# Seven block products for the output product of the 64-wide heads, and normed rows kept in DRAM

## The chip, the core and the metric

The kernel runs on one core of one Trainium2 chip. The metric is the device time of one execution in microseconds (us); the time of a kernel is the median of its runs.

## What is computed

The reference is a decoder of two layers on `x` of 8 entries x 256 rows x 256 columns, all in 32-bit floats. Each of six stages adds its result to `x`, and each works on the row-normed `x`. The change touches the last two stages:

```python
# fifth stage: cross attention, 16 heads of 64, 256 keys of a context plus one null key
q = _split_heads(x_normed @ Wq); k, v = split(context @ Wkv)      # plus the null key and value in front
attn = softmax(q * scale @ k.T)
out = (attn @ v) merged to 1024 columns
out = out @ Wout                                                   # 256 x 1024 times 1024 x 256, per entry
x = x + layernorm(out, 1e-6) * ln_scale + ln_bias
# sixth stage: one of 8 experts per row, and a shared expert for all rows, on the normed x
x = x + silu(x_n @ ws1) * (x_n @ ws3) @ ws2 + routed(x_n)
```

## The kernel before

Tensors are kept with 128 partitions. `x` stays in SBUF as 16 tiles of 128 rows. An entry is two such tiles.

The fifth stage (`null_cross_attention`) is a loop over the 8 entries. For entry b, TensorE forms the scores (`stx`), ScalarE their exponentials (`pTx`), TensorE the value products (`ox`) and the sums (`den`), and the result stands transposed in `oT`, 1024 columns of the heads as 8 chunks of 128 partitions by 256 tokens. Beside it, keys, values and queries for entry b + 1 are made by `seven`, which forms a 2 x 2 block product as seven block products with Strassen-like sums. Its two PSUM banks, `xb` and `yb`, are summed into and read several times on the way; a third, `zb`, is used once. The sums of the weights (`tw`, `twq`) are made once at the start of the stage by `sums_of_weights`; the sums of the rows (`sw`, `swq`) once per entry by `sums_of_rows`. The generators `k7`, `v7` and `q7` yield after each block product, so that they can be interleaved by hand.

The division of `oT` by the sums goes through DRAM: VectorE makes the reciprocals, four small DMAs on SP write them (`rd`), two DMAs of 512 KB read them back repeated over partitions (`rs`), and `divide` multiplies on GpSimd (in the last entry on GpSimd and VectorE). Then `outward` forms the output product as a plain product: per token tile, one null-value product and eight chunk products into one `mm` buffer, read by one copy:

```python
for t in range(2):
    product(ps[:, t, :], en[:, cols], nvw, True, False)
    for c in range(nc8):
        product(ps[:, t, :], oT[:, c, cols], wout_x[:, c, :], False, c == nc8 - 1)
nc.scalar.copy(y, ps)
```

`product` issues one matmul for each half of 64 output partitions; the profile records two passes for each. After `outward` come the norm statistics of `y`, the affine part, and the sum into `x`.

For the sixth stage each entry's finished `x` is normed (`routed_norm`), turned (`routed_rows`) into its slice of one tile `xnTe` (16 KB on each partition, in the pool `ws` opened before the stage) and multiplied by the router (`routed_scores`). In the last entry there are no keys to make, so the pools of the projection (`wproj`: the context tile, `wkv_x` and `wq_x`, the keys `kT` and values `vx`, the weight sums) are closed. `load_shared` then opens the pool `mids` in their place and loads the shared expert's weights `ws13`; `w_out` loads `ws2`. TensorE fills the place of the seven products with the first hidden products of the shared expert, `hx` (`hidden_shared(0)`, six steps, on rows 0 and 1 of `xnTe`), four of them ahead of the last `outward` and two behind it. `hidden_seven` follows for rows 2 and 3.

The order on TensorE is written out by hand within `manual_schedule`; on VectorE, ScalarE, GpSimd and SP a scheduler chooses it in this stage, and every engine and DMA queue works in order. PSUM here has three buffers `mm` of one bank, two buffers `sc` of two banks (`stx`, the bank pairs of `seven`, `hx`) and one for `den`. A tile reuses memory only once all users of what stood there have ended.

Of the kernel before, what the change touches and what calls it, by code (L numbers as in the profile page):

```python
# [29 lines left out]
F32 = mybir.dt.float32  # L30
# [4 lines left out]
ALU = mybir.AluOpType  # L35
# [122 lines left out]
def plain(  # L158
# [123 lines left out]
    def transposed(rows, work, mm, tag, dst=None, bufs=2):  # L282

        ps = mm.tile([P, 2, 2 * P], F32, tag="mm", name="tr")
        for t in range(2):
            for c in range(2):
                nc.tensor.transpose(ps[:, c, t * P : (t + 1) * P], rows[:, t, c * P : (c + 1) * P], ident)
        if dst is None:
            dst = work.tile([P, 2, 2 * P], F32, tag=tag, name=tag, bufs=bufs)
        nc.scalar.copy(dst, ps)  # L290
        return dst
# [815 lines left out]
    def w_in(pool, src1, src3, name):  # L1107

        t = pool.tile([P, 2, 2 * FF + tail], F32, name=name, tag=name)
        nc.sync.dma_start(t[:, :, :FF], src1.rearrange("(c p) f -> p c f", p=P))  # L1110
        nc.sync.dma_start(t[:, :, FF + tail :], src3.rearrange("(c p) f -> p c f", p=P))
        nc.gpsimd.tensor_copy(t[:, :, FF : FF + tail], t[:, :, 2 * FF :])
        return t

    def ended(t):

        nc.gpsimd.memset(t[tail:, full, :], 0.0)
        return t
# [12 lines left out]
    def load_router():  # L1131
        router = pool_s.tile([P, 2, E], F32, name="router")
        nc.gpsimd.dma_start(router, a["L1_ffn_router_DE"].rearrange("(c p) e -> p c e", p=P))
        shared.update(router=router, xnT=pool_s.tile([P, 2, B * S], F32, name="xnTe"))

    def load_shared(pool):

        shared["ws13"] = w_in(pool, a["L1_ffn_ws1_DF"], a["L1_ffn_ws3_DF"], "ws13")

        shared["mid_s"] = [ended(pool.tile([P, NFC, 2 * S], F32, name=f"mid{i}")) for i in range(2)]  # L1140
        shared["ws2"] = ended(pool.tile([P, NFC, D], F32, name="ws2"))

    def hidden(mid, first, n, pair, silu):

# [134 lines left out]
        return xn  # L1279

    def routed_rows(b, xn, work):
        transposed(xn, work, mm, "", shared["xnT"][:, :, bass.ts(b, S)])

    def routed_scores(b):

        ps = mm.tile([P, 2, D], F32, tag="mm", name="sc")
        for t in range(2):
            for c in range(2):
                product(
                    ps[:, t, :E], shared["xnT"][:, c, bass.ts(2 * b + t, P)], shared["router"][:, c, :], c == 0, c == 1  # L1290
                )
        nc.vector.tensor_copy(sc[:, 2 * b : 2 * b + 2, :], ps[:, :, :E])  # L1292

# [76 lines left out]
    def null_cross_attention(phase):  # L1370
# [18 lines left out]
        def w_blocks(w, m, extra):  # L1389

            v = w.rearrange("p (j c) (m k f) -> p j c m k f", j=2, m=m, k=2)
            blocks = [[v[:, j, :, :, k, :] for k in range(2)] for j in range(2)]
            t1, t2, t4 = (extra[:, i] for i in range(3))
            return blocks, (t1, t2, blocks[0][1], t4)
# [2 lines left out]
        kv_blocks = w_blocks(wkv_x, 2, wsum.tile([P, 3, *shape], F32, name="tw"))  # L1397
        shape = D // P // 2, 1, XH * XD // 2
        q_blocks = w_blocks(wq_x, 1, wsum.tile([P, 3, *shape], F32, name="twq"))

        def sums_of_weights(blocks, which):
            ((b11, b12), (b21, b22)), (t1, t2, t3, t4) = blocks
# [5 lines left out]
        def w_terms(blocks, m):  # L1408

            ((b11, b12), (b21, b22)), (t1, t2, t3, t4) = blocks  # L1410
            return [t[:, :, m, :] for t in (b11, b21, b22, t4, t1, t2, t3)]

        def sums_of_rows(rows, n, name, apart):


            def block(i, j):
                return rows[:, n * j : n * (j + 1), bass.ts(i, P)]

            sw = wsum.tile([P, 4 if apart else 3, n, P], F32, tag=name, name=name)
            s1, s2, s4 = (sw[:, i] for i in range(3))  # L1420
            s3 = sw[:, 3] if apart else block(1, 0)
            nc.vector.tensor_tensor(s1, block(1, 0), block(1, 1), ALU.add)
            nc.vector.tensor_tensor(s2, s1, block(0, 0), ALU.subtract)
            nc.vector.tensor_tensor(s4, block(0, 1), s2, ALU.subtract)
            nc.vector.tensor_tensor(s3, block(0, 0), block(1, 0), ALU.subtract)
            return block(0, 0), block(0, 1), s4, block(1, 1), s1, s2, s3
# [182 lines left out]
                    oT[:, c2 : c2 + 2, :], oT[:, c2 : c2 + 2, :], rs[:, c2 : c2 + 2, :], ALU.mult  # L1609
                )  # L1610

        def outward(b, oT, en):
            y = work.tile([P, 2, D], F32, tag="y", name="yx", bufs=1)
            ps = mm.tile([P, 2, D], F32, tag="mm", name="wo")
            for t in range(2):
                cols = bass.ts(t, P)
                product(ps[:, t, :], en[:, cols], nvw, True, False)
                for c in range(nc8):
                    product(ps[:, t, :], oT[:, c, cols], wout_x[:, c, :], False, c == nc8 - 1)
            nc.scalar.copy(y, ps)  # L1620
            mv, rs = norm_stats([y[:, t, :] for t in range(2)], 1e-6, small, "lx")
            for t in range(2):
                xt = x[:, 2 * b + t, :]
                normed(y[:, t, :], y[:, t, :], mv, rs, t)
                nc.vector.tensor_tensor(y[:, t, :], y[:, t, :], lns, ALU.mult)
                nc.vector.tensor_tensor(y[:, t, :], y[:, t, :], lnb, ALU.add)
                nc.gpsimd.tensor_tensor(xt, xt, y[:, t, :], ALU.add)
# [14 lines left out]
        (kT, v), qT = kv0, query_room()  # L1642
        sums_of_weights(kv_blocks, slice(0, 3))
        sums_of_weights(q_blocks, slice(0, 3))
        en = null_key(xnT)
        features(qT, wq_x, xnT, nc.vector.tensor_copy)
        for blocks in (kv_blocks, q_blocks):
# [3 lines left out]
        for b in range(B):  # L1651
            more = b + 1 < B
            if more:
                ctxT = context(b + 1)
            oT, den, rest = weighted(kT, v, qT)
            if more:
                _, xnT = layernorm_T(b + 1, work, mm, 1)
                if b:
                    xe = routed_norm(b - 1, work)
                of_ctx = sums_of_rows(ctxT, CTX // P // 2, "sw", False)  # L1660
            else:
                xe = routed_norm(b - 1, work)
                rest()

                wproj.close()
                late = ctx.enter_context(tc.tile_pool(name="mids", bufs=1, side="right"))
                tables = ctx.enter_context(tc.tile_pool(name="route", bufs=1, side="right"))
                load_shared(late)
                sums = phase.enter_context(tc.tile_pool(name="sums", bufs=1, side="right"))
                order.enter_context(tc.manual_schedule(engines={mybir.EngineType.PE}))  # L1670
            if more:
                order.enter_context(tc.manual_schedule(engines={mybir.EngineType.PE}))
            if b:
                routed_rows(b - 1, xe, work)
            if more:
                of_x = sums_of_rows(xnT, 1, "swq", True)
                kT, v, qT = key_room(), value_room(), query_room()
                k7 = seven("k7", of_ctx, w_terms(kv_blocks, 0), kT, False)
                v7 = seven("v7", of_ctx, w_terms(kv_blocks, 1), v, True)
                q7 = seven("q7", of_x, w_terms(q_blocks, 0), qT, False)  # L1680
                next(k7)
                rest()
            rs, old = reciprocals(b, den, en), en
            if b == 1:
                in_range()
            if not more:
                w_out(shared["ws2"], a["L1_ffn_ws2_FD"])
                routing_tables(tables)
            if more:

                for made in (k7, k7, v7, k7, k7, k7, v7, v7, q7, v7, q7, v7, v7, q7):
                    next(made)
            else:
                first = hidden_shared(0, pair, lambda n: spare()[:, 0, :n])
                for i in range(4):
                    next(first)
                    if i == 0:
                        routed_scores(b - 1)
                shared["of_w"] = sums_of_shared(*(sums.tile([P, full * P], F32, name=f"tws{i}") for i in range(4)))
            divide(oT, rs, (nc.gpsimd, nc.gpsimd if more else nc.vector))  # L1700
            outward(b, oT, old)
            if more:
                next(q7), next(q7)
                if b:
                    routed_scores(b - 1)
                next(q7)
                en = null_key(xnT)
            else:
                for _ in first:
                    pass  # L1710
            order.close()
# [1230 lines left out]
```

## Time and profile before

| | us |
|---|---|
| Median of 3 runs | 1150.59 (1148.03 to 1150.82) |
| The profiled execution's own time | 1146.4 |
| Its span | 1144.7 |
| Its mean granted TensorE clock | 0.993 of full |
| TensorE matmul busy | 1106.4 (97%) |
| VectorE, ScalarE, GpSimd busy | 581.4, 444.9, 418.8 |
| First matmul of the fifth stage to the first of the expert stage | 439.1 to 923.0 |

The span runs from the first to the last recorded work of the execution; 1.7 us lie around it. A timeline line gives the start and the duration in us, the engine, the source line, the operation, output<-input by the program's names, and the number of instructions merged into it. Matmuls are pipelined, so a line's duration runs a little beyond the start of the next. `SPq` is the queue that SP issues DMAs from. A window line gives its bounds and length, busy time and count for each engine, the granted clock, the DMA engines' share and GB/s.

### The profile page before, as it was taken

To read this page: it belongs to the slowest core of one execution; us is meant where nothing else is said; L and a number is where in the kernel's file an instruction comes from. 1 tells how busy PE (TensorE), PEld (TensorE's weight loads), DVE (VectorE), ACT (ScalarE), POOL (GpSimd) and SP (SyncE) were. 2 spreads that over 40 slices of the span, in tenths; PEclk is the share of its full clock that TensorE was granted. 3 is DMA by queue.
4 is the path that set the end of the run, shared out by engine and by line. 5 is a ranking of instruction groups with operands and counts; after the bars stand their busy time and mean duration, and the time that the engine had idled before them with its cause. 6 is when DMAs were issued, how large, how long until landed. Compare 5 with 4: busy or idle time off the path is not lost.

```text
span 1144.7 us, 33720 instructions
## 1 busy us (share of the span) xinstructions
PE 1106.4 (97%) x14690; PEld 704.9 (62%) x14690; DVE 581.4 (51%) x1577; ACT 444.9 (39%) x699; POOL 418.8 (37%) x480
## 2 busy tenths in 40 slices
PE   6979999999999999999999999999999999999997
PEld 3434455555555445767676767676765667888874
DVE  5557889899878447343433333332324573222213
ACT  4757776656444432232323323232414220222320
POOL 2427366446677422324141414142425223000014
PEclk9989999999999999999999999999999999999999
DMA  8073333231103200101010101010103026799934
GB/s 246 2 240 121 105 107 96 71 112 54 37 11 143 109 3 19 40 19 39 20 40 19 39 20 40 19 39 19 40 20 95 1 94 262 312 415 386 390 107 141
DMA packets 52253, 117.15 MB, mean 102 GB/s; under 512 B 8816, under 2 KB 37216, under 8 KB 47744
## 3 DMA queue, kind: packets, MB, share of 16 engines
q1 hardware_dynamic: 45920, 99.17, 25.4%
q0 software_dynamic: 3456, 12.73, 3.1%
q10 hardware_dynamic: 2720, 3.02, 0.7%
q8 instruction: 117, 1.92, 0.7%
q14 instruction: 40, 0.33, 0.1%
HBM read 104.26 MB, written 27.93 MB: 115 GB/s over the span
## 4 chain that ended last, share of the span: by engine, by line
PE 86%; DVE 6%; ACT 3%; issue 1%; SPq 1%; DMA 1%; POOL 1%; ACTq 0%; DVEq 0%; POOLq 0%
PE h L272 7%; PE st L330 7%; PE k L272 7%; PE v L272 6%; PE wo L272 5%; PE o L367 5%; PE ox L1553 5%; PE stx L1513 5%; PE out L1930 4%; PE out L1747 4%; PE qk L278 3%; PE h L1161 3%; PE q L272 3%; ACT pT L341 2%; PE ao L278 2%; PE v L278 2%
## 5 line engine op out<-in xcount | busy, mean ns | idle before, releaser
L341 ACT ACTIVATE pT<-st 128x1024 f32<-128x1024 f32 (+1 forms) x128 | 110.5, 915 | 74.2 <-PE st L330 70.3
L367 PE MATMUL o<-pT,padv 128*32 128x256 f32 (+1 forms) x1536 | 96.4, 367 | 7.0 <-DVE by_q L383 5.5
L1519 POOL TENSOR_TENSOR both<-pTx 128x512 f32<-128x512 f32 x64 | 81.5, 1298 | 27.1 <-issue 23.8
L272 PE MATMUL h<-xrT,w 128*64 128x128 f32 (+1 forms) x1936 | 87.1, 250 | 0.5 <-issue 0.5
L272 PEld LDWEIGHTS h<-xrT,w 128*64 128x64 f32 x1936 | 84.6, 137 | 3.4 <-issue 1.1
L341 ACT ACTIVATE pT<-st,kbias 128x1024 f32<-128x1024 f32 x64 | 67.9, 1112 | 36.0 <-PE st L330 36.0
L1154 DVE TENSOR_TENSOR midr<-sl,h 128x128 f32<-128x128 f32 x102 | 29.4, 288 | 100.7 <-PE h L272 67.5
L367 PEld LDWEIGHTS o<-pT,padv 128*32 128x32 f32 x1536 | 44.6, 110 | 54.4 <-issue 18.9
L1517 ACT ACTIVATE pTx<-stx 128x1024 f32<-128x1024 f32 x64 | 62.1, 1022 | 40.7 <-PE stx L1513 35.7
L1153 ACT ACTIVATE sl<-h 128x128 f32<-128x128 f32 (+1 forms) x114 | 35.4, 311 | 94.8 <-PE h L272 55.8
L330 PE MATMUL st<-qm,kT 32*128 32x512 f32 (+1 forms) x512 | 67.3, 594 | 3.7 <-DVE seq L513 2.2
L254 POOL TENSOR_TENSOR lnrs<-lnve,mhalf 128x2 f32<-128x2 f32 x48 | 35.8, 749 | 91.8 <-DVE lnve L252 84.9
L278 PE MATMUL qk<-xnT,l_wqkv 128*32 128x256 f32 x1024 | 68.5, 391 | 0.0
L1513 PE MATMUL stx<-qTx,kTx 64*128 64x256 f32 x512 | 64.3, 391 | 2.5 <-ACT pTx L1517 2.5
L1553 PE MATMUL ox<-pTx,vx 128*32 128x256 f32 x1024 | 62.3, 380 | 0.0
L1608 POOL TENSOR_TENSOR oT<-oT,rs 128x512 f32<-128x512 f32 x30 | 37.7, 1287 | 65.7 <-DMA rs<-rd 65.7
L1513 PEld LDWEIGHTS stx<-qTx,kTx 64*128 64x128 f32 x512 | 46.1, 186 | 20.7 <-ACT pTx L1517 7.2
L272 PE MATMUL wo<-wout_x,oT 128*64 128x256 f32 x512 | 58.0, 379 | 0.0
L346 POOL TENSOR_SCALAR_AFFINE_SELECT pT<-pT 128x512 f32<-128x512 f32 x64 | 42.1, 672 | 41.4 <-ACT pT L341 41.1
L254 POOL TENSOR_TENSOR lxrs<-lxve,mhalf 128x2 f32<-128x2 f32 x8 | 5.6, 704 | 133.5 <-DVE sc L1292 103.3
L278 PEld LDWEIGHTS qk<-xnT,l_wqkv 128*32 128x32 f32 x1024 | 32.9, 113 | 26.9 <-issue 8.7
L1930 PE MATMUL out<-w,midr 128*64 128x256 f32 x408 | 47.5, 379 | 0.7 <-issue 0.7
(365 smaller groups left out, 2154.8 us busy)
## 6 DMA issues: line engine op xcount, KB each, us to landing
w<-packs SPq DMA_DIRECT2D x22, 1408.0 KB
w<-packs SPq DMA_DIRECT2D x22, 768.0 KB
rs<-rd SPq DMA_DIRECT2D x16, 512.0 KB
packs<-L_ffn_w_eDF SPq DMA_DIRECT2D x8, 704.0 KB
packs<-L_ffn_w_eDF SPq DMA_DIRECT2D x8, 640.0 KB
packs<-L_ffn_w_eFD SPq DMA_DIRECT2D x8, 640.0 KB
wkv_x<-L_xattn_Wkv POOLq DMA_DIRECT2D x1, 4096.0 KB, 16.9
ctxT<-ctx_T SPq DMA_DIRECT2D x8, 512.0 KB
```

Of the source, the lines that this page charges most:

```text
L272: nc.tensor.matmul(out[h], lhsT[:, h], rhs, start=start, stop=stop, skip_group_check=True)
L278: nc.tensor.matmul(out[h : h + HP], lhsT[:, h : h + HP], rhs, start=start, stop=stop, skip_group_check=True)
L330: nc.tensor.matmul(st[:, r, :, :n], self.kT[rows, c, bass.ts(kt, P)], self.qm[rows, :, c, q0:], start=True, stop=True,)
L341: nc.scalar.activation(pT[:, :, :, :n], st[:, 2 * k : 2 * k + 2, :, :n], AF.Exp, scale=self.scale, **kb)
L346: nc.gpsimd.affine_select(out=pT[:, :, :, :P], in_=pT[:, :, :, :P], compare_op=ALU.is_ge, fill=0.0, base=0, pattern=[[0, 2], [0, 2], [1, P ...
L367: nc.tensor.matmul(o[HP * j : HP * j + HP, m, q0:], self.v_pad[:, kt, 8 * c + 2 * j + m, :], pTs[j // 2][:, j % 2, m, : S - q0], start=kt ...
L1513: nc.tensor.matmul(st[:, g, kt, :], kT[rows, c, bass.ts(kt, P)], qT[rows, c, :], start=True, stop=True)
L1517: nc.scalar.activation(pT, st, AF.Exp, scale=scale)
L1519: nc.gpsimd.tensor_tensor(both, pT[:, :, 0, :], pT[:, :, 1, :], ALU.add)
L1553: nc.tensor.matmul(o[at : at + HP, i, :], v[:, kt, 2 * (c2 + i) + g, lo : lo + HP], pT[:, g, kt, :], start=kt == 0, stop=kt == 1, skip_gro ...
L1747: nc.tensor.matmul(ps, mid[:, i, lo : lo + P], w2[:, i, :], start=i == 0, stop=i == NFC - 1)
L1930: nc.tensor.matmul(ps[h], mid[:, i, h], sets[k % len(sets)][1][:, i, :], start=i == 0, stop=i == NFC - 1, skip_group_check=True,)
```

## The change

The output product of each entry is made as seven products of blocks of 128 tokens x 512 inner columns x 128 output columns, in place of the eight that a plain product takes. The sums of the weight blocks (`two`, 16 VectorE sums of 128x128, with four of them written in place into `wout_x`) are made once at the start of the stage; the sums of the row blocks (`swo`, one of them in place in `oT`) once per entry on VectorE. The null-value products go into blocks 2, 5, 3 and 4, with the difference `ed` of two halves of `en` for block 3. The blocks use one `sc` buffer (`xb`, `yb`) and one `mm` buffer (`zb`), with three small copies on ScalarE, three sums on VectorE, and a last copy. Between blocks 7 and 4 stands one product of other work, `between()`: a step of `q7`, or in the last entry the fifth hidden step.

The turned normed rows of entries 0 to 5 go into a small tile `xnk` and from it to a DRAM tile `xt`, 256 KB each, on SP's queue. The tile `xnTe` is opened in the pool `mids` in the last entry, and six DMAs on SP bring the rows back, after the two of `ws13`. Entries 6 and 7 are copied straight into it. In that pool the two `mid` tiles are now opened first.

```diff
 def load_router():
-    shared.update(router=router, xnT=pool_s.tile([P, 2, B * S], F32, name="xnTe"))
+    shared["router"] = router
+xt = dram.tile([B - 2, P, 2, S], F32, name="xt")
+rows_of = {}
 def load_shared(pool):
+    mids = [pool.tile([P, NFC, 2 * S], F32, name=f"mid{i}") for i in range(2)]
     shared["ws13"] = w_in(pool, a["L1_ffn_ws1_DF"], a["L1_ffn_ws3_DF"], "ws13")
-    shared["mid_s"] = [ended(pool.tile([P, NFC, 2 * S], F32, name=f"mid{i}")) for i in range(2)]
-    shared["ws2"] = ended(pool.tile([P, NFC, D], F32, name="ws2"))
+    ws2 = pool.tile([P, NFC, D], F32, name="ws2")
+    xnT = pool.tile([P, 2, B * S], F32, name="xnTe")
+    for b in range(B - 2):
+        nc.sync.dma_start(xnT[:, :, bass.ts(b, S)], xt[b])
+    shared["mid_s"] = [ended(t) for t in mids]
+    shared["ws2"], shared["xnT"] = ended(ws2), xnT
 def routed_rows(b, xn, work):
-    transposed(xn, work, mm, "", shared["xnT"][:, :, bass.ts(b, S)])
+    if b < B - 2:
+        rows_of[b] = transposed(xn, work, mm, "xnk", bufs=1)
+        nc.sync.dma_start(xt[b], rows_of[b])
+    else:
+        rows_of[b] = transposed(xn, work, mm, "", shared["xnT"][:, :, bass.ts(b, S)])
...
+shape = nc8 // 2, 1, D // 2
+o_blocks = w_blocks(wout_x, 1, work.tile([P, 3, *shape], F32, name="two", bufs=1))
...
-def outward(b, oT, en):
+def outward(b, oT, en, between):
+    s_terms = sums_of_rows(oT, nc8 // 2, "swo", False, work)
+    t_terms = w_terms(o_blocks, 0)
...
+    nc.gpsimd.tensor_tensor(ed, en[:, :P], en[:, P:], ALU.subtract)
+    xy = scp.tile([P, 2, 2 * S], F32, tag="sc", name="wo")
+    xb, yb = xy[:, 0, :P], xy[:, 1, :P]
+    zb = mm.tile([P, 2 * S], F32, tag="mm", name="woz")[:, :P]
...
+    kept = work.tile([P, 3, P], F32, tag="pT", name="wok", bufs=4)
+    p1, p5, u = (kept[:, i] for i in range(3))
+    product_of(1, xb, True)
+    reads(xb, nc.scalar.copy(p1, xb))
+    product_of(2, zb, True, (e1, n1))
+    nc.vector.tensor_tensor(y[:, 0, :P], p1, zb, ALU.add)
+    product_of(5, yb, True, (e2, n2))
+    reads(yb, nc.scalar.copy(p5, yb))
+    product_of(6, xb, False)
+    reads(xb, nc.scalar.copy(u, xb))
+    product_of(3, yb, False, (ed, n2))
+    nc.vector.tensor_tensor(y[:, 0, P:], u, yb, ALU.add)
+    product_of(7, xb, False)
+    reads(xb, nc.vector.tensor_tensor(y[:, 1, P:], p5, xb, ALU.add))
+    between()
+    product_of(4, xb, False, (e2, n1))
+    nc.scalar.copy(y[:, 1, :P], xb)
...
 sums_of_weights(q_blocks, slice(0, 3))
+sums_of_weights(o_blocks, slice(0, 4))
 en = null_key(xnT)
 features(qT, wq_x, xnT, nc.vector.tensor_copy)
...
-outward(b, oT, old)
+outward(b, oT, old, lambda: next(q7 if more else first))
 if more:
-    next(q7), next(q7)
+    next(q7)
```

## The prediction

> **What bounds it.** I read the page's busy shares and chain first, then the timeline of each engine around the edited stage, then the order and waits of the changed program as built.
>
> ```profile
> PE 1106.4 (97%) x14690; PEld 704.9 (62%) x14690; DVE 581.4 (51%) x1577; ACT 444.9 (39%) x699; POOL 418.8 (37%) x480
> PE 86%; DVE 6%; ACT 3%; issue 1%; SPq 1%; DMA 1%; POOL 1%; ACTq 0%; DVEq 0%; POOLq 0%
> ```
>
> TensorE is busy 97% of the span and is 86% of the chain. In the stage of the heads of 64 (439 to 922 us) it hardly idles, so one us of TensorE removed there is worth one us, and one us of TensorE idleness added costs one. The timeline of TensorE, first in entry 0, then at the output product of entry 1:
>
> ```profile
> 470.23 3.66 PE L272 MATMUL k<-sw,tw 128*64 128x128 f32 x64
> 473.73 1.89 PE L272 MATMUL v<-wkv_x,ctxT 128*64 128x512 f32 x8
> ```
> ```profile
> 553.12 0.60 PE L272 MATMUL wo<-nvw,en 128*64 128x256 f32 x4
> 553.55 3.62 PE L272 MATMUL wo<-wout_x,oT 128*64 128x256 f32 x32
> 557.00 0.60 PE L272 MATMUL wo<-nvw,en 128*64 128x256 f32 x4
> 557.43 3.62 PE L272 MATMUL wo<-wout_x,oT 128*64 128x256 f32 x32
> 560.89 1.92 PE L272 MATMUL q<-swq,wq_x 128*64 128x128 f32 x32
> ```
>
> Columns: start, duration, engine, line, operation, count. Starts give the pitch: 64 matmuls of 128 columns take 473.73 - 470.23 = 3.50 us, 54.7 ns each; the 72 of the output product, 256 columns wide, take 560.89 - 553.12 = 7.77 us, 107.9 ns each.
>
> **Part 1, the product itself.** 7 block products x 4 chunks x 2 column halves x 2 recorded passes are 112 matmuls, the four null-value blocks 16 more: 128 x 54.7 ns = 7.00 us. That is 0.77 us less in each of 8 entries: **-6.2 us**. Against this the Trainium skill, page "TensorE: Matmul & The Clock Gate", section "Back-to-back issue gap", gives about 81 ns for a sustained 128-column matmul with its weight load; by it 128 would take 10.4 us and each entry would lose 2.6 us. The row above is for the same shape in the same loop, and decides.
>
> What the blocks need lies beside other work. In entry 1 the division by the sums ends on GpSimd at 543.06; the built order puts the first of the four row sums on VectorE (128x512, 0.60 to 0.69 us like the other 512-wide sums) just behind it, ahead of `vx<-v7p,v7z`, which slips from 541.24 to about 543.8. Behind it on VectorE the next copy was due at 547.35, and nobody on TensorE waits for the slipped one (three buffers in `mm`). The other sums end near 546.2, while the first block starts at 553.12: cost nothing; without the gap of 547.35 it would be 2.5 us an entry. The first block reuses the bank pair of `v7`, whose last copy ends at 553.05: 0 to 0.1 us an entry, I take 0. Each later bank read has a whole block product (0.87 us) between it and the next write of that bank; small copies take 0.3 us. `between()` puts one `q` product ahead of block 4, and the last `q` product no longer waits 0.38 us for `qTx` in entry 0: **-0.4 us** with entry 0 alone. The store of normed rows stands on SP between `ctxT` and `rd`; the rows are copied by 525.26, a sibling 256-wide issue takes about 0.5 us, `rd` is issued at 529.37: nothing.
>
> **Part 2, the sums of `wout_x` at the start of the stage.** Sixteen VectorE sums of 128x128 now stand ahead of the first `qTx` copy:
>
> ```profile
> 439.98 8.76 PE L272 MATMUL fm<-xnT,wq_x 128*64 128x256 f32 x64
> 448.68 2.00 PE L1513 MATMUL stx<-qTx,kTx 64*128 64x256 f32 x16
> ```
> ```profile
> 444.85 0.69 DVE L1406 TENSOR_TENSOR twq<-wq_x 128x512 f32<-128x512 f32 x1
> 445.45 0.69 DVE L1384 COPY qTx<-fm 128x512 f32<-128x512 f32 x1
> ```
>
> The fourth `fm` tile needs the first's buffer. Before, that copy came at 445.45 to 446.14, and the fourth tile began near 448.75 - 1.73 = 447.0 with no idleness. After: 444.85, three `twq` sums at 0.60 us, sixteen small ones at 0.20 to 0.31 us (starts of the `swq` rows at 466.77 to 467.49; I take 0.23, most do not depend on their neighbour), then the copy of 0.69: 444.85 + 1.8 + 3.7 + 0.7 = 451.05. TensorE idles **4.05 us** (3.5 to 5.3).
>
> An idle TensorE costs more than the gap. The windows of the first us, with the granted clock third from last:
>
> ```profile
> 18.00:20.00 2.00, 0.04 (x4) 0.04 (x4) 1.90 (x6) 1.43 (x3) 0.62 (x2) 1.00 1.09 367
> 20.00:22.00 2.00, 2.00 (x12) 0.50 (x16) 1.86 (x10) 0.98 (x4) 0.00 (x0) 0.54 1.09 351
> 22.00:24.00 2.00, 2.00 (x25) 0.89 (x24) 0.31 (x2) 1.88 (x2) 0.70 (x1) 0.60 1.10 358
> 24.00:26.00 2.00, 2.00 (x28) 0.72 (x24) 0.40 (x1) 1.10 (x3) 0.00 (x0) 1.00 1.02 376
> ```
>
> After 2.15 us of idleness the clock is about a half for some 3.8 us of work; the same shows after the 5.50 us wait that ends at 81.12 (half until 85.0) and after the short stalls at 436.6 to 439.1 (half from 440.0 to about 443.8). So each new gap of this size costs about 3.8 x 0.5 = **1.9 us** more, and nothing where the gap misses. The skill's page, section "Part 1: The HAM clock gate", has a window of about 3.4 us to fall and to recover, which would make this 1.7 us; the trace fell after a shorter gap. Part 2: 4.05 + 1.9 = **+6.0 us**.
>
> **Part 3, the shared rows in entry 7.** `xnTe` moves into the pool of the shared expert, beside `ws13` and ahead of it the two `mid` tiles. The pool grows past the region of `wkv_x` into that of `kT` and `vx`. In the program as built, the load of `ws13` waits for the last value product (`ox`) of entry 7; before, it waited for a `q` product of entry 6 and was issued here:
>
> ```profile
> 855.33 0.40 SPq L1110 DMA_DIRECT2D ws<-L_ffn_ws_DF  x1
> ```
> ```profile
> 872.50 1.91 PE L1553 MATMUL ox<-pTx,vx 128*32 128x256 f32 x32
> 874.22 0.61 PE L1528 MATMUL den<-both,hot 128*32 128x256 f32 x8
> 874.77 0.66 PE L287 MATMUL tr<-ident,xne 128*128 128x128 f32 x4
> 875.26 3.60 PE L1161 MATMUL hx<-xnTe,ws 128*128 128x512 f32 x8
> ```
>
> `ox` ends near 874.4; the hidden product `hx`, which needs `ws13` and rows 0 and 1 of `xnTe`, stands at 875.26. So 20 us of cover are gone. The price, from the load of before, by windows (last column GB/s):
>
> ```profile
> 855.00:857.00 2.00, 2.00 (x42) 1.83 (x40) 1.43 (x6) 0.19 (x1) 1.50 (x4) 1.00 0.20 41
> 857.00:859.00 2.00, 2.00 (x20) 1.45 (x18) 1.51 (x5) 0.98 (x3) 0.45 (x1) 1.00 0.92 329
> 859.00:861.00 2.00, 1.68 (x16) 1.05 (x14) 1.12 (x4) 1.74 (x2) 1.47 (x2) 1.00 1.03 405
> ```
>
> By 861 they sum to 2 x (41 + 329 + 405) = 1550 KB; `ws13` is 1442 KB, there 5.4 us after issue. Rows 0 and 1 are 524 KB in 1 KB pieces, like `ctxT` (325 GB/s in its best us): 1.6 us. Landing to use is 0.7 us (`ctxT` ends near 555.35 and is used at 556.07). Ready at 874.45 + 5.4 + 1.6 + 0.7 = 882.15: **6.9 us** idle (5 to 8.5), then the half clock, **1.9 us**.
>
> `rd` and `rs` stand on SP behind these loads and wait for their semaphores: `rd` complete near 885.5, `rs` behind rows 2 to 5 and `ws2` starts near 887, and moves 5 us as before, landing near 893; the division lets block 1 start at 894.5 and block 2 at 896. TensorE, with 4 hidden steps (14.5 us) and the slow clock, arrives at 898.6: nothing, but 0 to 4 us if that queue is slower. In the tail the sixth hidden step waits for `mid` of the fifth, one block of 1.09 us ahead instead of 7.8 us of product: 0.2 + 0.6 + 0.65 - 1.09, about **0.5 us**. The last rows' norm has 9.6 us for a chain of about 8.5: nothing.
>
> **Sum.** -6.2 - 0.4 + 6.0 + 6.9 + 1.9 + 0.5 = **+8.7 us**: on the profiled execution's span of 1144.7, 1153.4; its own time of 1146.4 becomes 1155.1. The three timed runs have their median 4.2 us above that execution; I add the change to the median: 1150.6 + 8.7 = **1159.3 us**. What a measurement can tell from no change is 0.3%, 3.5 us.
>
> **Rivals.** A (not slower): the last stage's loads cost little. If they land within the 0.8 us between `ox` and `hx`, Part 3 is the 0.5 us of the tail alone and the sum is -0.1: 1150.5. It decides while idleness and clock loss there stay below 3.6 us together (-0.1 + 3.6 = 3.5). For it: the wait on `ox` is a matter of pools, not of bytes, and eight queued loads may overlap. Against: 1442 KB took 5.4 us in this very trace. 10%. B (slower still): `rs` becomes the next wait; divisions start 4 us later than reckoned, TensorE waits about 3 us, with no further clock loss: 1162.3. 15%. C: the seven products do not get 54.7 ns. With three banks and reads between, 0.4 us lost in each entry makes 3.2 us: 1162.5. For it: margins of 0 to 0.1 us at the bank of `v7`. 12%. D (faster by over 0.3%): both gaps shrink below half, -6.6 + 3: 1147.0; needs rows that nothing here shows. 3%. The forecast (1155.5 to 1162) holds 60%.
>
> **Range.** Low end: gaps of 3.5 and 5 us, one without the clock loss, -6.6 + 3.5 + 5 + 1.9 + 0.5 = +4.3, rounded down towards A: 1154. High end: 5.3 + 1.9 + 8.5 + 1.9 + 0.5 - 6.6 = +11.5, with B's 3 us: 1165. The chances: slower by over 0.3%, B, C, nearly all of the forecast and a part of A: 0.87; within 0.3% 0.10; faster 0.03.
>
> **What would show it.** The changed profile should have the `wo` block products at about 55 ns each and 7.0 us an entry without idle between; a gap ahead of the last `fm` tile, released by `qTx`, of 4 us; SP issuing `ws13` after the last `ox`; a gap of about 7 us ahead of the first `hx`, released by a DMA; a granted clock near 0.5 behind both gaps; no gap at block 1 in entry 7. I am wrong if either gap is under 2 us, if the clock stays at 1.0, or if `wo` has idleness of its own in each entry.

## The result and the profile after

| | before | after |
|---|---|---|
| median, us | 1150.82 (1148.03 to 1152.2) | 1166.53 (1163.56 to 1168.11) |
| ratio | | 1.0135, interval 1.0114 to 1.0156 |
| the profiled execution, us | 1146.4 | 1168.11 |

The change makes the kernel 15.5 us slower (0.0135 x 1150.6). The direction was forecast, the size not: the forecast was 1159.3 us, its range ended at 1165.

Each trace here is one execution. It is cut on TensorE at fixed places: the first `nps` of the fifth stage, the first `stx` of entries 1 and 7, the first `wo` of entry 7, the first `out`, and TensorE's end.

| stretch, us | forecast of the change | before | after | difference |
|---|---|---|---|---|
| opening and entry 0 | +4.8 | 67.45 | 72.86 | +5.4 |
| entries 1 to 6 | -4.6 | 351.04 | 350.17 | -0.9 |
| entry 7 up to `wo` | +8.8 | 32.30 | 41.92 | +9.6 |
| `wo` of entry 7 to `out` | -0.3 | 33.13 | 34.16 | +1.0 |
| expert stage | 0 | 215.21 | 216.56 | +1.4 |

The forecast's column regroups its terms: 6.0 - 0.77 - 0.4, six times -0.77, 6.9 + 1.9, and 0.5 - 0.77. The fifth stage is 15.2 us longer against 8.7 forecast. Most of what was missed stands in one row: six entries that should have saved 4.6 us save 0.9. The two executions lie 21.6 us apart, more than the medians. 16.5 us of that stand in these rows; the rest lies outside them, 2.7 us ahead of the fifth stage and 2.4 us behind TensorE's last product, and no experiment here looked into it.

The waits view of TensorE in the changed kernel (total, times, longest) has three waits of over 1 us for another engine or a DMA that the kernel before does not have:

```profile
PE hx L1169 <- DMA xnTe<-xt: 6.8, 1, 6.8
...
PE fm L272 <- DVE qTx L1396: 5.3, 1, 5.3
...
PE wo L272 <- DVE yx L1666: 3.6, 8, 0.5
```

The first two are the forecast gaps. The third occurs once in each of the 8 entries and is in no term of the forecast's sum. TensorE's timeline at the output product of entry 1:

```profile
561.10 1.09 PE L272 MATMUL wo<-wout_x,oT 128*64 128x128 f32 x16
562.00 1.07 PE L272 MATMUL woz<-wout_x,oT 128*64 128x128 f32 x16
...
565.05 1.07 PE L272 MATMUL wo<-wout_x,swo 128*64 128x128 f32 x16
565.93 0.42 PE L272 MATMUL wo<-nvw,ed 128*64 128x128 f32 x4
566.79 1.09 PE L272 MATMUL wo<-wout_x,oT 128*64 128x128 f32 x16 [0.45 <-DVE yx L1666]
567.72 1.04 PE L272 MATMUL q<-swq,wq_x 128*64 128x128 f32 x16
```

Sixteen matmuls follow each other in 0.87 to 0.90 us, 54 to 56 ns each, as the forecast took them. But block 7, the line at 566.79, waits for the VectorE sum of line 1666, which reads bank `yb`. Block 7 writes `xb`. The two banks are one tile, so a read of either holds back a write of the other unless the pair is declared independent. `outward` does that for the reads given to its helper `reads`, and the read of line 1666 is the one that is not given to it. From start to start the null product takes 0.86 us instead of 0.22.

The opening, on TensorE and on VectorE:

```profile
442.69 5.35 PE L272 MATMUL fm<-xnT,wq_x 128*64 128x256 f32 x48
453.34 3.68 PE L272 MATMUL fm<-xnT,wq_x 128*64 128x256 f32 x16 [5.30 <-DVE qTx L1396]
```
```profile
450.18 1.70 DVE L1420 TENSOR_TENSOR two<-wout_x,two 128x128 f32<-128x128 f32 x8
451.79 0.89 DVE L1420 TENSOR_TENSOR wout_x<-wout_x 128x128 f32<-128x128 f32 x4
452.60 1.88 DVE L1396 COPY qTx<-fm 128x512 f32<-128x512 f32 x3
```

The copy that frees the first `fm` tile stands behind all sums, and starts at 452.60 where it started at 445.45 before. The sixteen matmuls behind the gap take 3.68 us, where three times as many took 5.35 just before. The windows give the reason in their third column from the end, the granted clock:

```profile
448.00:450.00 2.00, 0.04 (x2) 0.00 (x0) 2.00 (x7) 0.00 (x0) 0.00 (x0) 1.00 0.00 0
450.00:452.00 2.00, 0.00 (x0) 0.00 (x0) 2.00 (x12) 0.00 (x0) 0.00 (x0) 0.76 0.00 0
452.00:454.00 2.00, 0.66 (x4) 0.47 (x6) 2.00 (x7) 0.00 (x0) 0.00 (x0) 0.50 0.00 0
454.00:456.00 2.00, 2.00 (x14) 1.05 (x12) 2.00 (x4) 0.00 (x0) 0.00 (x0) 0.50 0.00 0
```

In entry 7, TensorE and SP's queue:

```profile
881.41 0.61 PE L1542 MATMUL den<-both,hot 128*32 128x256 f32 x8
881.96 0.65 PE L287 MATMUL tr<-ident,xne 128*128 128x128 f32 x4
889.39 6.34 PE L1169 MATMUL hx<-xnTe,ws 128*128 128x512 f32 x8 [6.78 <-DMA xnTe<-xt]
```
```profile
881.70 0.40 SPq L1110 DMA_DIRECT2D ws<-L_ffn_ws_DF  x1
882.16 0.46 SPq L1111 DMA_DIRECT2D ws<-L_ffn_ws_DF  x1
882.66 3.98 SPq L1146 DMA_DIRECT2D xnTe<-xt  x6
```

```profile
884.00:886.00 2.00, 0.00 (x0) 0.00 (x0) 1.60 (x4) 0.00 (x0) 1.84 (x7) 0.63 1.04 407
890.00:892.00 2.00, 2.00 (x3) 0.67 (x2) 1.93 (x5) 0.00 (x0) 0.00 (x0) 0.50 1.06 262
```

The load of `ws13` is issued 17 us behind entry 7's first scores (864.81), where it stood 2 us ahead of them before. The same eight hidden matmuls that took 3.60 us take 6.34, the first 5.4 us of it at half the clock. `rs` lands in time: `wo` at 906.73 waits for nothing, so rival B did not come.

### The profile page after: what moved, and what is told of

Same layout as the page of the kernel before. It is cut to its first block, busy times and chain, and to the rows that moved or that the text cites. A ratio compares the mean times of both kernels' runs of the same rounds, so it can differ in the third digit from the quotient of the medians.

```text
span 1166.3 us, 34767 instructions
## 1 busy us (share of the span) xinstructions
PE 1107.6 (95%) x15138; PEld 723.8 (62%) x15138; DVE 609.6 (52%) x1649; ACT 448.9 (38%) x723; POOL 422.7 (36%) x488
## 3 DMA queue, kind: packets, MB, share of 16 engines
q8 instruction: 121, 1.98, 0.7%
## 5 line engine op out<-in xcount | busy, mean ns | idle before, releaser
L1575 DVE COPY oT<-ox 128x512 f32<-128x512 f32 x16 | 11.1, 692 | 84.2 <-PE ox L1567 84.2
L383 DVE STREAM_TRANSPOSE by_q<-o 128x512 f32<-128x512 f32 x48 | 34.0, 708 | 28.2 <-PE o L367 28.1
```

## The experiments

My theory after the result: three separate waits, each with a cause of its own that can be taken away without touching the arithmetic, plus the clock behind two of them, make up the loss. The rival: the narrow products, or the rows in DRAM, cost time in themselves. The stretches of each trace, with the ratios to the kernel before:

| kernel | ratio (interval) | opening, entry 0 | entries 1 to 6 | entry 7 to `wo` | tail | expert |
|---|---|---|---|---|---|---|
| before | 1 | 67.45 | 351.04 | 32.30 | 33.13 | 215.21 |
| after | 1.0135 (1.0114 to 1.0156) | 72.86 | 350.17 | 41.92 | 34.16 | 216.56 |
| bank read named | 1.0083 (1.0066 to 1.0099) | 71.39 | 346.11 | 42.21 | 33.49 | 216.46 |
| late sums | 1.0100 (1.0085 to 1.0114) | 68.39 | 350.20 | 41.69 | 34.17 | 216.64 |
| two pools | 1.0083 (1.0068 to 1.0099) | 73.54 | 350.15 | 33.64 | 34.16 | 217.28 |
| rows alone | 1.0077 (1.0057 to 1.0097) | 66.84 | 351.06 | 41.28 | 33.14 | 214.82 |
| all three edits | 1.0011 (0.9998 to 1.0024) | 67.30 | 346.08 | 33.65 | 33.48 | 216.47 |
| sums apart | 0.9990 (0.9977 to 1.0003) | 65.58 | 346.12 | 32.80 | 36.25 | 217.57 |
| sums apart, reordered | 0.9956 (0.9941 to 0.9971) | 65.59 | 346.09 | 32.23 | 34.11 | 218.50 |

### The bank read named

```diff
-nc.vector.tensor_tensor(y[:, 0, P:], u, yb, ALU.add)
+reads(yb, nc.vector.tensor_tensor(y[:, 0, P:], u, yb, ALU.add))
```

> Changed kernel, with the VectorE read of bank yb (L1666) named as a read of that bank, so that block product 7, which writes the other bank, does not wait for it; nothing is left out. Theory (the seven products lose their gain to this one wait): the trace of the changed kernel shows PE wo waiting 3.6 us in 8 entries for yx L1666, and 0.64 us an entry from start to start; without it -3.6 to -5.1 us, so about 1162 us, ratio to the kernel before 1.009 to 1.0105, and the seven entries 0 to 6 shrink from 405.2 to about 401 us. Rival (the wait only takes the place of another: the copies on ScalarE of u and p5, or narrow products that are slow in themselves): less than 1 us, 1166, ratio 1.013, with the same 0.45 us ahead of block 7 put down to ScalarE.

Measured: 1.0083, 6.0 us less than the changed kernel ((1.0135 - 1.0083) x 1150), against 3.6 to 5.1 expected. Six entries go from 350.17 to 346.11 us, 0.68 each. Block 7 of entry 1 now stands right behind the null product, and nothing takes the place of the wait:

```profile
560.88 0.42 PE L272 MATMUL wo<-nvw,ed 128*64 128x128 f32 x4
561.10 1.07 PE L272 MATMUL wo<-wout_x,oT 128*64 128x128 f32 x16
```

An entry now takes (351.04 - 346.11) / 6 = 0.82 us less than in the kernel before; the forecast had 0.77. The rival falls: the narrow products are as fast as reckoned.

### The sums of wout_x later

```diff
-sums_of_weights(o_blocks, slice(0, 4))
 en = null_key(xnT)
 features(qT, wq_x, xnT, nc.vector.tensor_copy)
 for blocks in (kv_blocks, q_blocks):
     sums_of_weights(blocks, slice(3, 4))
+sums_of_weights(o_blocks, slice(0, 4))
```

> Changed kernel, with the sixteen sums of wout_x put behind the features of x and the last sums of the other two weights, so that no copy of fm tiles to qTx waits for them on VectorE; nothing is left out. Theory (the gap of 5.3 us ahead of the last fm tile and the half clock after it are the whole price of the sums): -6.0 us, about 1160.5 us, ratio 1.008; the opening shrinks from 17.9 to about 11.9 us, with half the clock at its start as in the kernel before. Rival 1 (the clock's dip is only moved, so that what goes is the gap less what the moved dip costs): -3.5 us. Rival 2 (the 3.6 us of sums are late somewhere else, ahead of the normed rows and row sums of entry 1): -2 to -4 us, with a new wait of TensorE in entry 0.

Measured: 1.0100, 4.0 us less; the stretch shrinks by 4.5. The gap ahead of the last `fm` tile is gone, and two smaller things are left. The clock is at a half at 440 to 443 us, as in the kernel before, and the sums now make the copies of `oT` late in entry 0, which the waits view shows:

```profile
PE tr L287 <- DVE oT L1575: 1.5, 1, 1.5
```

From the first `nps` to the first `stx` the kernel gives 5.6 us back (15.17 us in the changed kernel, 9.60 here, 9.61 before), and the new wait takes 1.5 of it. So rival 2 holds, and the theory's 6.0 was 2 us too much.

### The mid tiles in a pool of their own

```diff
-mids = [pool.tile([P, NFC, 2 * S], F32, name=f"mid{i}") for i in range(2)]
+mids = [of_mids.tile([P, NFC, 2 * S], F32, name=f"mid{i}") for i in range(2)]
...
-late = ctx.enter_context(tc.tile_pool(name="mids", bufs=1, side="right"))
+late = ctx.enter_context(tc.tile_pool(name="late", bufs=1, side="right"))
+beside = ctx.enter_context(tc.tile_pool(name="mids", bufs=1, side="right"))
```

> Changed kernel, with the two mid tiles in a pool of their own behind that of ws13, ws2 and the rows, so that ws13 lies in a pool over regions that are free after entry 6's last q product and its load need not wait for the last value product of entry 7; nothing is left out, and the same bytes are loaded. Theory (the wait of the pool and the half clock after it are the price of the rows in DRAM): -6.8 us of gap and -2.7 of clock, about 1157 us, ratio 1.0055; the stretch from the first stx of entry 7 to its output product shrinks from 41.9 to about 32.4 us. Rival 1 (1.6 MB of rows and the loads of ws13 cost the queue time wherever they stand: rs comes late): a wait of 2 to 4 us ahead of block 1 or 2 in entry 7 stays, 1160. Rival 2 (loads that run beside entry 7 slow its other transfers and copies): 1 to 2 us more in entry 7's scores.

Measured: 1.0083, 6.0 us less by the ratios; in the trace entry 7 shrinks by 8.3, while the opening and the expert stage are 0.7 us longer each. SP issues the load two us ahead of entry 7's first scores (863.12), and the first hidden product runs at the full clock, without a wait for its data:

```profile
861.02 0.40 SPq L1110 DMA_DIRECT2D ws<-L_ffn_ws_DF  x1
```
```profile
882.16 3.60 PE L1169 MATMUL hx<-xnTe,ws 128*128 128x512 f32 x8
```

The bytes, their number of DMAs and their order are the same: it was the pool, not the transfer. Entry 7 is still 1.3 us longer than before, which the kernel with all three edits explains below.

### The rows alone

The kernel before, with the rows in DRAM and the late pool of the change, and the plain product.

> The kernel before with one part of the change: the normed rows kept in DRAM and the mid tiles, ws13, ws2 and the rows in one late pool, but the output product plain, in eight blocks, without the sums of wout_x. Nothing is left out. Theory: only entry 7 pays, 6.8 us of gap and 2.7 of clock, so ratio 1.008 (1.007 to 1.009), with the opening and entries 0 to 6 as in the kernel before. In the expert stage TensorE's queue holds as many instructions as before (6335 ahead of the first out, against 6333), so if the two stalls of 1.4 us that all kernels with the new product show there (put down to issue) come from the place in that queue, this one has 0.7 and 0.5 us as before; if they come from the rows or the pools, it has 1.4 and 1.4. Rival (the rows cost nothing but the wait is the product's): ratio 1.000.

Measured: 1.0077, as expected. Entry 7 is 9.0 us longer, everything else within 0.6 of the kernel before. The gap ahead of the hidden product is 6.8 us, and the product takes 5.62 us instead of 3.60, so the clock costs 2.0 us here and not 2.7. Of the expected stalls in the expert stage there is one, of 0.55 us.

### The gap filled

```diff
+fill = mm.tile([P, 2, 2 * P], F32, tag="mm", name="fill")
+for i in range(56):
+    nc.tensor.matmul(fill[:, 0, :P], ident, ident, start=i == 0, stop=i == 55)
 first = hidden_shared(0, pair, lambda n: spare()[:, 0, :n])
```

> Changed kernel with 56 small products (128x128 of the identity, into a spare PSUM tile that nobody reads) put on TensorE between the transposes of entry 6's normed rows and the first hidden product of entry 7, where the changed kernel idles 6.8 us; the load of ws13 stands where it stood. They compute nothing that is wanted; nothing is left out. At 0.11 us each they fill some 6.2 us. Theory (the gap's second price is the clock): the first hidden product starts where it did, about 15 us after the last ox, but runs at the full clock: 3.6 us instead of 6.3, so the stretch from the first stx of entry 7 to its output product shrinks from 41.9 to about 39.2 us and the kernel by 2.7 us, ratio about 1.011. Rival (the slow product has to do with its freshly loaded data or with the transfers beside it, not with idleness): 6.3 us again, and 41.9.

Measured: 1.0158 (1.0139 to 1.0177), no faster than the changed kernel; entry 7 up to `wo` takes 44.74 us against 41.92. The size of the filling was wrong, the reason for the clock right:

```profile
880.06 12.67 PE L1748 MATMUL fill<-ident 128*128 128x128 f32 x112
892.56 3.60 PE L1169 MATMUL hx<-xnTe,ws 128*128 128x512 f32 x8
```

A pass with 128 output columns of weights takes 12.5 / 112 = 112 ns, not the 55 ns of the passes with 64 that I had reckoned with, and the filling ran 5.6 us past the gap. With half of it:

> The changed kernel with 28 filling products in the gap ahead of the first hidden product of entry 7, half of the earlier number, since each recorded pass of such a 128x128 product took 112 ns there and 56 of them 12.5 us. They compute nothing that is wanted; nothing is left out. Theory (idleness brings the half clock): they take 6.2 us, the first hidden product starts within 0.8 us of where it starts in the changed kernel and takes 3.6 us instead of 6.3, so from the first stx of entry 7 to its output product 39.2 us instead of 41.9, and the kernel gains 2.7 us: ratio about 1.011. Rival (a gap of under a microsecond, or the filling products themselves, bring the half clock as well): 6.3 us again.

```profile
880.41 6.42 PE L1748 MATMUL fill<-ident 128*128 128x128 f32 x56
887.20 3.67 PE L1169 MATMUL hx<-xnTe,ws 128*128 128x512 f32 x8 [0.38 <-issue]
```
```profile
888.00:890.00 2.00, 2.00 (x6) 0.91 (x5) 1.93 (x5) 0.00 (x0) 0.00 (x0) 1.00 0.91 274
```

Measured: 1.0115 (1.0088 to 1.0143), and 39.10 us for entry 7 up to `wo`, against 39.2 expected and 41.92 in the changed kernel. The data come no earlier, the same loads run beside it, and the hidden product still takes 3.67 instead of 6.34 us. So in this trace the gap itself, and not the data or the transfers, costs the 2.7 us, and useless work buys them back. In the kernel's time the gain is 2.3 us by the ratios, with intervals that overlap.

### All three edits, and what was left

> Changed kernel with all three edits: the read of yb named, the sums of wout_x late, the mid tiles in a pool of their own. Nothing is left out. Theory (the three waits and the clock behind two of them are all that the change costs): 1166.5 - 5 - 6 - 9.5 = 1146 us, that is 4 to 5 us faster than the kernel before, ratio 0.996. Rival (the narrow products or the rows in DRAM cost time by themselves): no faster than before, 1150 to 1154 us, ratio 1.000 to 1.003.

Measured: 1.0011, level with the kernel before and not 4 to 5 us faster. The number is the rival's. Within the noise it is what the three gains come to (1.0135 - 0.0052 - 0.0035 - 0.0052 = 0.9996), so the question is what the narrow products' 6 us still pay for. `both` is GpSimd's sum of two halves of the exponentials, from which TensorE makes the sums `den`. The groups of GpSimd and VectorE beside entry 7's scores in this kernel (count, then busy us and the mean ns of one, then idle time):

```profile
L1533 POOL TENSOR_TENSOR both<-pTx 128x512 f32<-128x512 f32 x8 | 12.9, 1647 | 0.0
```
```profile
L1181 DVE TENSOR_TENSOR tws<-ws,tws 128x640 f32<-128x640 f32 x2 | 3.7, 1838 | 0.0
...
L1193 DVE TENSOR_TENSOR sx<-xnTe 128x256 f32<-128x256 f32 x1 | 1.5, 1500 | 0.0
```

and the same two kinds in the kernel before, where the sums stand behind the scores:

```profile
L1519 POOL TENSOR_TENSOR both<-pTx 128x512 f32<-128x512 f32 x8 | 10.1, 1287 | 0.1
```
```profile
L1173 DVE TENSOR_TENSOR tws<-ws,tws 128x640 f32<-128x640 f32 x2 | 1.6, 782 | 0.0
...
L1185 DVE TENSOR_TENSOR sx<-xnTe 128x256 f32<-128x256 f32 x1 | 0.4, 417 | 0.0
```

With its weights there early, the scheduler had put VectorE's sums of two SBUF tiles beside GpSimd's additions `both`. The two slow each other: a VectorE sum from 0.42 to 1.50 us, an addition from 1.29 to 1.65. In entry 0 an addition takes 1.98 us on the mean, against 1.43 in the kernel before, and that is mostly a single one (the shortest, the median and the longest in ns):

```profile
L1533 POOL TENSOR_TENSOR both<-pTx x8: 1271/1452/6078, 448.5 to 462.8; 128x512 f32<-128x512 f32 x8
```

It starts at 448.5, while VectorE adds without a break until 453.4 (the late sums at 0.28 us each), and takes 6.08 us. TensorE pays 1.0 us in entry 0 and 0.5 and 0.3 in entry 7. The Trainium skill, page "SBUF — State Buffer", section "SBUF: two separate sides", says that GpSimd and VectorE share one pair of ports, that a VectorE operation with two SBUF inputs needs it beside a GpSimd operation that reads SBUF, and that whoever comes second waits for the whole instruction. The rows of entry 7 agree: 1.50 is the sum's own 0.42 and most of an addition's 1.29. The addition of 6.08 us goes further: it is as long as the rest of that run of sums and its own time, not of one sum. The next kernel moves the sums away. Those of `wout_x` stand among entry 0's block products, where GpSimd has no additions to make, and those of the shared expert behind entry 7's first hidden products; VectorE's order is written by hand there:

```diff
-sums_of_weights(o_blocks, slice(0, 4))
...
+        for i, made in enumerate((k7, k7, v7, k7, k7, k7, v7, v7, q7, v7, q7, v7, v7, q7)):
+            next(made)
+            if b == 0 and 5 <= i < 9:
+                sums_of_weights(o_blocks, slice(i - 5, i - 4))
```

> The kernel with all three edits, with VectorE's sums moved away from GpSimd's: the sums of wout_x stand among the block products of entry 0 (after the copies of kT) instead of beside entry 0's scores, and those of ws13 and of the last rows behind the first hidden products of entry 7 instead of beside its scores. Nothing is left out. Theory (in the kernel with all three edits the additions both on GpSimd take 1.65 to 2.5 us instead of 1.26 to 1.5 while VectorE adds two SBUF tiles, whose own 128x256 sums take 1.5 us instead of 0.42, and TensorE waits for both 1.0 us in entry 0 and 0.45 in entry 7, and 0.26 for oT): both goes back to 1.26 to 1.5 us, these waits go, -1.7 us, so 0.998 to 1.000 of the kernel before. Rival (the additions are slow for another reason, such as the loads beside them): the same durations and waits as with all three edits, ratio 1.001.

Measured: 0.9990. The additions in entry 7's scores take 1.29 us again (in entry 0 1.55, beside the row sums `sw`), and the waits for `both` and `oT` are gone there: 65.58 and 32.80 us instead of 67.30 and 33.65. But the hand-written order had a fault of its own, in the tail:

```profile
PE wo L272 <- DVE oT L1624: 1.9, 1, 1.9
```

I had put the division of `oT` behind a product of VectorE, `mid`, that itself waits for TensorE's fourth hidden step. The last kernel puts it ahead:

> The kernel with the three edits and VectorE's sums moved away from GpSimd's, as before, but with VectorE's work of entry 7 put in another order: the division of oT now stands ahead of the product mid of the fourth hidden step, which in the earlier order made TensorE wait 1.9 us for oT and 0.5 for mid at the output product. Nothing is left out. Theory: both waits go and nothing takes their place, the tail shrinks from 36.25 to about 33.8 us and the kernel from 0.999 to 0.997 of the kernel before (0.9955 to 0.998), about 1143 us: faster by more than 0.3% or just about. Rival (TensorE then waits for the fourth mid, or for the sums swo): 1 to 2 us at blocks 1 to 5 of entry 7, and 0.998 to 0.999.

Measured: 0.9956 (0.9941 to 0.9971), 5.1 us faster than the kernel before and 20.6 faster than the changed kernel. Both waits are gone, and the tail takes 34.11 us, against 33.8 expected. It keeps both parts of the change, and beats both kernels. The gain over the kernel before is clear by the medians; the five stretches of the two traces add up to 2.6 us less, as 3.3 us in the expert stage go against it.

### A padded queue

The expert stage is untouched, but every kernel with the block products spends 1.2 to 3.3 us more in it than the kernel before. What differs there are stalls. The timelines show TensorE standing still there for nothing that the profile records, first before, then after:

```profile
1018.29 1.29 PE L1930 MATMUL out<-w,midr 128*64 128x256 f32 x9 [0.70 <-issue]
1039.90 1.09 PE L272 MATMUL h<-xrT,w 128*64 128x64 f32 x30 [0.54 <-issue]
```
```profile
1011.02 0.39 PE L272 MATMUL h<-xrT,w 128*64 128x64 f32 x5 [1.37 <-issue]
1083.41 0.86 PE L272 MATMUL h<-xrT,w 128*64 128x64 f32 x22 [1.37 <-issue]
```

Less these stalls the stage takes 213.8 to 214.3 us in eleven of the twelve traces, whichever kernel (the twelfth, the one with the shorter filling, has a wait of 1.5 us for `mid` besides).

> The kernel before with 235 products of one column (of the identity, into a spare PSUM tile that nobody reads) in entry 7, so that TensorE's queue holds exactly as many instructions ahead of the first out as in the changed kernel (6568); they cost time where they stand, and only the expert stage is read. Nothing is left out. Theory (the stalls put down to issue belong to places in the instruction queue): h stalls twice for 1.3 to 1.4 us, about 70 and 142 us after the first out, as in the changed kernel. Rival (they belong to the rows, the pools or the product): 0.7 us at 95 and 0.5 us at 117, as in the kernel before.

Measured, in a single execution: one stall of 1.34 us, 69.6 us after the first `out`; none at 142, 95 or 117. The place of the first moved as the theory says. The second did not come. The shorter filling, with 28 products more than the changed kernel, has stalls at 95, 117 and 167, and the rows alone just 0.55 us at 117. So the block products are not needed for the stall at 70, and the rows and pools do not bring the pair at 70 and 142. That the stalls go with the program on TensorE's queue fits all this and is not shown. By which rule they fall, and how long they last, stays open.

## Why the prediction was right in direction and short in size

**The step that failed** is in Part 1: "Each later bank read has a whole block product (0.87 us) between it and the next write of that bank". That is true of each bank by itself. It says nothing of the other bank, and block 7 waits for a read of the other bank, a wait that the sum put at nothing. It costs 0.68 us an entry by the stretches, 5.4 us in eight. With it named, one edit of one line gives 6.0 us back by the ratios. The forecast's own sign of being wrong, `wo` with idleness of its own in each entry, came. Of the forecast's 6.6 us for the product, the changed kernel kept 6.6 - 5.4 = 1.2. Rival C had priced it as 0.4 us an entry and named "three banks and reads between" as the place; it got 12%, because the margins were argued from the bank written and not from the tile that both banks share.

**The rate of the products** was right. The forecast set its row of 54.7 ns against the Trainium skill's 81 ns; 16 matmuls in 0.87 us are 54.4 ns. The page "TensorE: Matmul & The Clock Gate", section "LDWEIGHTS (loading the stationary operand)", gives a weight load as its columns divided by 1.2, in ns; an estimate from it is 53 for 64 columns and 107 for 128. Passes with 128 moving columns took 54 and 112 here. It is not the whole rule, since the time also follows the moving columns: a pass with 64 weight columns took 107.9 ns with 256 of them, and one with 128 weight columns 450 with 512 (3.60 us for 8).

**Part 2** was right in its mechanism and came out at +5.4 with entry 0's product, against +4.8. Its gap was 5.30 us and not 4.05, and not because VectorE took longer: counted from `nps`, the copy started 10.8 us on (452.60 - 441.78), 0.5 earlier than reckoned. TensorE was there 1.7 us earlier, because the half clock of the kernel before at 440 us, which I had read as fixed, is missing in this execution. It is there in five of the twelve traces and missing in seven; where it falls on the first three `fm` tiles, the wait behind them is 3.6 us instead of 5.3. The whole hardly changes: from the first `nps` to the first `stx` it is 15.17 us with the longer gap and 15.18 in the two-pools kernel, which has the dip and the shorter gap, since the copy sets when the fourth tile can start. Against 9.61 before, that is 5.6 us, near the forecast's 6.0. So the gap was mis-sized and the sum right partly by luck.

**Part 3** was right: 6.78 us against 6.9, and the rows alone at 1.0077 confirm it. The clock was mis-sized, 2.74 us against 1.9. The half clock lasted from 884.5 to 894.7, the first part of it in the gap, and 5.4 us of it fell on work; the term had been taken from 3.8 us of work. The same gap of 6.8 us cost 2.5 us of clock with the late sums and 2.0 with the rows alone, so 1.9 is near the low end of what a gap of this size cost here.

**The tail** was forecast at -0.77 + 0.5 and came to +1.0. The wait for `mid` was 0.17 us instead of 0.5. In its place stand block 7's wait and 0.75 us for a copy on ScalarE, which is queued behind an activation that waits for VectorE, which has the norm of `y` to finish first. The expert stage's 1.4 us were in no term.

**Where the forecast's and the result's sums part:** entries 1 to 6 3.7 us, opening 0.6, entry 7 0.8, tail 1.3, together 6.4 of the 15.2 in the fifth stage; and 1.4 in the expert stage.

## What to carry to other kernels

When a tile holds several PSUM banks, list every read of the tile against every later write of it, not bank by bank, and read in the built program what each product waits for. When buffers are opened in the place of closed pools, the first load waits for the last user of anything that the whole pool reaches: open what is wanted early in a pool of its own. A freed load lets the scheduler move other work forward, so look again at what VectorE's two-input sums then stand beside.

## What the runs showed of the hardware

Back-to-back work is not enough for the full clock. In the padded queue, 470 recorded passes of one column ran for 95.75 us with TensorE recorded busy throughout, 204 ns apart on the mean. The clock was full for the first 5 us and then stood at a half until other work had run for 5 us:

```profile
874.59 95.75 PE L1696 MATMUL fill<-ident 128*128 128x1 f32 x470
```
```profile
876.00:878.00 2.00, 2.00 (x20) 2.00 (x20) 2.00 (x3) 0.00 (x0) 0.66 (x1) 1.00 0.00 0
900.00:902.00 2.00, 2.00 (x11) 2.00 (x11) 0.00 (x0) 0.00 (x0) 0.00 (x0) 0.50 0.00 0
```

The passes of the shorter filling, with 128 moving columns and just as dense, kept it at 1.00.

The same short stalls lose the clock in one execution and not in the next. Near 438 us, behind stalls of 1.04 and 0.80 us, the clock fell in five of twelve traces, near 290 us in four others. How long it stays down goes in steps: added up over windows of 2 us, a stretch of half clock lasts 3.4, 6.8 or 10.2 us in all twelve traces (95.6 us, 28 steps of 3.41, in the padded queue), leaving out what runs past TensorE's last product. So the clock's price is half of the half-clock time that is left when work resumes, and for gaps of 6.8 to 7.0 us in entry 7 it came to 2.0 to 2.9 us.

Half clock lasts 6.8 us in the trace of all three edits and 13.7 us in that of the kernel before, worth at most 3.4 and 6.9 us. These two executions lie 2.4 us apart (1144.0 and 1146.4), so a single trace may flatter that kernel while its median (1148.0 against 1146.7) does not.
